# A perceiver layer on one core: attention scores taken in two halves, softmax sums from a separate product with ones

## The chip, the core and the metric

The kernel runs on one core of a Trainium2 chip. The metric is device time in microseconds of one execution, as the median of several runs. Five engines work side by side, each through its own queue in order: TensorE (PE, matmuls; its weight loads are listed as PEld), VectorE (DVE), ScalarE (ACT), GpSimd (POOL) and SyncE (SP, which here only issues DMAs). Matmuls write to PSUM, eight banks of 512 float32 values per partition; DVE and ACT read it there.

## What is computed

64 samples, each with 64 tokens of 256 features (x) and a context of 256 tokens (ctx). Cut to what matters here:

```python
def xattn(queries, ctx):            # 16 heads of 16 features
    q = (queries @ Wq.T + bq).reshape(B, L, H, E)
    k = (ctx @ Wk.T + bk).reshape(B, S, H, E)
    v = (ctx @ Wv.T + bv).reshape(B, S, H, E)
    scores = einsum('blhe,bshe->bhls', q, k)
    attn = softmax(scores * E ** -0.5, axis=-1)
    return einsum('bhls,bshe->blhe', attn, v).reshape(B, L, H * E) @ Wo.T + bo

x = x + xattn(layernorm(x), ctx)
x = x + causal_self_attention(layernorm(x))
x = x + ffn(layernorm(x))           # gate, up, down; integer weights and rows
```

All attention matmuls are in float32.

## The kernel before

Everything is written as operations in a graph (`Graph.op`, L165): engine, a planned duration, a due time (`at`), what is read and written, and a function that emits the instructions. `Graph.run` (L214) then plays a list schedule with those planned durations. At each step it lets the operation start that can start first, among those due soon (`AHEAD`), by due time and a few penalties (`LATE`, `TURN`). The order it finds is the order of each engine's queue. `SHIFT` and `LAST` (L126, L145) move due times by kind of operation. Buffers come from rings with so many slots (`RINGS`, L1071); an operation that needs a buffer waits until a slot is free. Semaphores are placed afterwards, from what each instruction reads and writes.

The samples are cut into nine groups (seven of 8, two of 4). For each pair of samples, `project` (L585) makes keys and values from the context (`keys` L511, `values` L517; matmuls at L491 and L526). For each sample, `cross` (L594) does the cross-attention. For each group, `prepare` (L563) normalises x and makes the queries; when the group's samples are done, `self_attention` (L709) and `ffn` (L865) follow, interleaved with the next group's cross-attention by due times.

One sample in `cross`, with 2 chunks of 128 features (`hg`, KC = 2) and 4 column or row tiles of 32 (`j`, NJ = 4). A tile of 32 features holds two heads, and the queries are stored twice, masked to one head or the other, so 128 query columns stand for 2 heads x 64 tokens.

1. `scT` (L614, PE): transposed scores of keys against queries, 2 chunks x 2 key blocks x 4 row tiles = 16 matmuls of 128 columns, into one PSUM buffer `sc` of four banks. The ring has one slot; `mm`, the ring of all other matmul outputs, has the other four banks.
2. `nm` (L623, DVE): one transposing reduce over all 2048 elements gives the maximum over 32 keys.
3. `larger` (L628, DVE, tile `msl`), `mtp` (L634, PE, a transpose) and `terms` (L645 to L649, DVE, tiles `less` and `mT`): the maximum per query, negated, and split into three bfloat16 terms with its rounding remainders.
4. `less` (L660, PE): bfloat16 matmuls with a selection matrix subtract the maxima from the scores in PSUM.
5. `exp` (L665, ACT), one per chunk, writes `PT`.
6. `av` (L673, PE): product with the values. The value tile is laid out per head as 16 value columns beside 16 columns of ones (the tiles `v_0`, `v_1` are filled with ones at L1049, and the copy at L532 writes only the value columns), so 32 weight columns give one head's result and its sum of probabilities at once. Each half of the query columns (`h`) has its own matmuls:

```python
nc.tensor.matmul(
    av.t[rows(j), h, hg, :],
    v.t[:, ((n % 2) * SC + s) * NP + hg * NJ + j, 2 * h:2 * h + 2, :].rearrange(
        "p a e -> p (a e)"),
    pT.t[:, hg, j, s, h * T:(h + 1) * T], start=(s == 0), stop=(s == SC - 1))
```

7. `keep` (L690) and `own` (L693) on ACT, `both` (L696) on POOL collect results and sums. `ratio` (L700, L701, DVE) moves the sums by 16 partitions with a shuffle and inverts them, and `yT` (L704, POOL) multiplies.

The self-attention scores (`ssc`, L747) use the same four-bank buffer `sc`, eight samples at a time; four masks (L759, DVE) read it.

Of the kernel before, what the change touches and what calls it, by code (L numbers as in the profile page):

```python
# [33 lines left out]
F32 = mybir.dt.float32  # L34
BF16 = mybir.dt.bfloat16
AF = mybir.ActivationFunctionType
# [10 lines left out]
NP = H // 2  # L47
# [50 lines left out]
class Op:  # L98
# [17 lines left out]
AHEAD = 6.1849  # L116
HURRY, SPURT = 3.4019, 8
WAIT = 2308970000.0
LATE = 0.0053
TURN = 3.4322  # L120
# [6 lines left out]
    "ACT exp": -1.4, "ACT hqT f": -5.46, "ACT hscaled f": 4.84, "ACT k a": -0.61, "ACT k s": 2.17,  # L127
    "ACT keep": 0.44, "ACT norm a": -1.22, "ACT norm f": 1.09, "ACT norm s": -0.51, "ACT own": 0.44,
    "ACT q a": -3.14, "ACT q s": 1.22, "ACT qT f": -23.19, "ACT rounded f": -0.4, "ACT sexp s": -0.94,
    "ACT silu f": -0.21, "ACT skeep s": 2.53, "ACT spT s": -1.53, "ACT turned a": -1.95,  # L130
    "ACT turned s": -0.14, "ACT up f": 1.2, "ACT v a": -0.19, "ACT v s": 1.1, "DVE bo r": -6.72,
    "DVE hq f": -0.63, "DVE hscales f": 3.5, "DVE larger": -1.95, "DVE mask s": -0.49, "DVE ratio": 0.94,
    "DVE smax s": 1.13, "DVE stats a": -2.59, "DVE stats f": -2.72, "DVE stats s": -1.327,
    "DVE stot s": 0.63, "DVE syT s": -1.42, "DVE terms": -1.95, "DVE wdown sums": -6.1,
    "DVE wup sums": -2.9, "DVE wup unit": 0.26, "DVE x a": -3.34, "DVE x f": -0.15, "DVE x s": 1.86,
    "PE av": 1.72, "PE bo r": -2.99, "PE down f": 0.54, "PE k s": -0.72, "PE mtp": -0.83, "PE o a": -0.97,
    "PE o s": 0.94, "PE q a": -0.32, "PE q s": -0.26, "PE qtp f": 3.25, "PE sav s": 1.22, "PE scT": 0.36,
    "PE ssc": -2.15, "PE turn a": -1.44, "PE v a": -0.32, "PE v s": 1.99, "PE wdown total": -3.1,
    "PE wgate total": -2.28, "PE wup total": -4.23, "POOL bias": 0.57, "POOL less s": -2.32,
    "POOL over s": 2.24, "POOL root a": -5.86, "POOL root f": -3.26, "POOL yT": 1.48, "SP hqT f": 4.97,  # L140
    "SP load wdown": -3.38, "SP load wk": 3.07, "SP load wq": 2.43, "SP load wup": -1.71, "SP load x": 2.01,
    "SP store": 4.49,
# [3 lines left out]
    "ACT hqT f": 5.73, "ACT hscaled f": -4.23, "ACT k s": -3.91, "ACT norm f": -4.37, "ACT norm s": -1.11,  # L146
    "ACT qT f": 22.14, "ACT rounded f": -3.05, "ACT skeep s": -6.38, "ACT spT s": -1.93,
    "ACT turned s": -2.39, "ACT up f": -1.39, "DVE hq f": 1.46, "DVE hscales f": 1.38, "DVE mask s": -1.14,
    "DVE q f": 2.07, "DVE smax s": -3.22, "DVE stot s": -2.49, "DVE syT s": -0.48, "DVE x f": 5.34,
    "PE down f": 5.04, "PE gate/up f": 3.79, "PE k s": 0.78, "PE q s": 0.23, "PE qtp f": -4.38,  # L150
    "PE stp s": -2.34, "POOL h f": 0.75, "POOL less s": 1.71, "POOL root f": 3.94,
}
END = 60.9419
# [7 lines left out]
class Graph:  # L161
# [52 lines left out]
    def run(self, emit=True):  # L214
# [13 lines left out]
        table, mode, landed = None, "", 0.0  # L228
# [27 lines left out]
        while len(done) < len(self.ops):  # L256
# [21 lines left out]
            for o in head.chain:  # L278
# [18 lines left out]
                if o.bytes:  # L297
                    landed = max(landed, t + 1900.0) + o.bytes / 330.0
# [40 lines left out]
def layers(nc, a, out, R, c):  # L339
# [6 lines left out]
    wk, wv, wq, wo, wqkv, wout = (Buf(t=c["w" + n]) for n in ("k", "v", "q", "o", "qkv", "out"))  # L346
    xs = [bufs("x", [P, GB[g] * T // P, D], f"x_{g}") for g in range(NG)]
    cTs, kTs, vs, qms, yTs = {}, {}, {}, {}, {}
    msl = [Buf(t=c[f"msl_{i}"][:, :, 0:3 * QB].rearrange("p a (b t) -> p a b t", t=3)) for i in range(2)]
    spread = [Buf(t=c[f"v_{i}"], shape=[P, 2 * SC]) for i in range(2)]  # L350
# [13 lines left out]
    def load_weights(at, w, name):  # L364
        op("SP", 60, at, f"load {name}", lambda: nc.sync.dma_start(w.t, a[name]), writes=[w],
           size=KC * D * 4 * P)
# [150 lines left out]
    def values(at, w, c0, src, name, v, i0, spread=False):  # L517

# [11 lines left out]
        def keep():  # L530
            if spread:
                nc.scalar.copy(v.t[:, i0 * NP:(i0 + k) * NP, 0::3, :],  # L532
                               pm.t[:, 0:k * D].rearrange("p (r h e) -> p r h e", h=2, e=E))
            else:
                nc.scalar.copy(v.t[:, i0:i0 + k, :],
                               pm.t[:, 0:k * D].rearrange("p (i d) -> p i d", d=D))

        op("PE", k * KC * pe(D) + 60, at, f"v {name}", emit, reads=[src, w], writes=[pm],
           holds=[] if spread else [v])
        op("ACT", act(k * D), at, f"v {name}", keep, reads=[pm], writes=[(v, i0)])  # L540
# [44 lines left out]
    def project(bp, at, step):  # L585

        kT = kTs[bp] = bufs("kT", [P, KC, 2 * S], f"kT_{bp}")
        v = vs[bp] = spread[bp % 2]
        for hg in range(KC):
            keys(at + step * hg, wk, 0, c["bk_c"][:, hg:hg + 1], cTs[bp], f"a{bp}", kT, hg)  # L590
        for i0 in (0, 2):
            values(at + step * (2 + i0 // 2), wv, 0, cTs[bp], f"a{bp}", v, i0, True)

    def cross(n, at):  # L594
# [5 lines left out]
        ms = msl[n % 2]  # L600
        sT = bufs("sc", [P, NJ, KC, S], f"scT_{n}")
# [7 lines left out]
        def scores():  # L609

            for hg in range(KC):
# [536 lines left out]
```

## Time and profile before

| what | value |
|---|---|
| median of 3 runs (lowest to highest) | 893.63 us (889.04 to 896.21) |
| the profiled execution's own time | 889.85 us |
| its span in the trace | 887.8 us |
| mean granted TensorE clock | 0.969 of full speed |
| ACT busy | 655.1 us, 74% |
| POOL busy | 428.5 us, 48% |
| share of the chain that ended last | PE 45%, DVE 37%, ACT 9%, POOL 3% |
| PE `k_a`, `v_a` busy | 126.0 us, 123.4 us |
| PE `scT`, `av` busy | 76.8 us, 71.3 us |
| DVE `nm` | 64 x 2307 ns, 147.6 us |

The profile is one execution. A group's row gives line, engine and operation, output and input by name, shapes and count; then busy microseconds and the mean of one in ns; then the idle time of the engine just before it and what ended that. Matmuls are pipelined, so the mean of one is its time from issue to result, and a block is shorter than count times mean. A busy PE is not a PE at its peak.

### The profile page before, as it was taken

How to read it: one execution, taken by the hardware profiler on the slowest of the kernel's cores; microseconds unless marked ns; L12 is line 12 of the kernel's file. 1: busy time of each engine (PE TensorE's matmuls, PEld its weight loads, DVE VectorE, ACT ScalarE, POOL GpSimd, SP SyncE). 2: the span in 40 equal slices, each digit the busy share in tenths (PEclk: the TensorE clock that was granted, in tenths of full speed). 3: DMA queues.
4: the chain of work that ended last, by engine and by line, in shares of the span. 5: the costliest groups of instructions: out<-in, count | busy, mean ns of one | idle time of the engine just before them, and what ended most of it. 6: DMA issues, size and time to landing. Idle time of an engine off the chain costs nothing.

```text
span 887.8 us, 26233 instructions
## 1 busy us (share of the span) xinstructions
PE 806.7 (91%) x11112; PEld 537.6 (61%) x11112; DVE 681.5 (77%) x1403; ACT 655.1 (74%) x1046; POOL 428.5 (48%) x633
## 2 busy tenths in 40 slices
PE   6988989989989999999999999999999998887866
PEld 4654656765557655676567655766566655666534
DVE  2567778777779967898589967898488768888775
ACT  2544556566987689877997689867787497857886
POOL 3423265424655245534475355534367136536764
PEclk8998999999999999999999999999899999989988
DMA  7121210010211221113121221012112030002111
GB/s 270 35 97 49 73 49 25 12 40 2 61 37 38 50 83 29 23 32 74 55 37 38 49 73 33 18 38 72 37 28 45 16 70 4 14 3 38 37 36 60
DMA packets 47876, 41.70 MB, mean 47 GB/s; under 512 B 39312, under 2 KB 39824, under 8 KB 47760
## 3 DMA queue, kind: packets, MB, share of 16 engines
q1 hardware_dynamic: 46176, 39.85, 16.7%
q8 instruction: 88, 1.44, 0.7%
q10 hardware_dynamic: 1584, 0.18, 0.1%
q14 instruction: 28, 0.23, 0.1%
HBM read 26.65 MB, written 4.19 MB: 35 GB/s over the span
## 4 chain that ended last, share of the span: by engine, by line
PE 45%; DVE 37%; ACT 9%; POOL 3%; issue 3%; DMA 3%; ACTq 0%; SPq 0%; POOLq 0%; DVEq 0%
DVE nm L623 8%; PE k_a L491 8%; PE scT L614 5%; PE v_a L526 5%; DVE s_s L759 3%; DVE smax_s L762 3%; PE q_a L491 3%; ACT PT L665 3%; PE av L673 3%; DVE stot_s L770 3%; DVE less L648 3%; PE k_s L491 3%; PE down_f L944 2%; DVE less L647 2%; DVE keep L701 2%
## 5 line engine op out<-in xcount | busy, mean ns | idle before, releaser
L623 DVE TRANSPOSE_TENSOR_REDUCE nm<-scT 128x64 f32<-128x2048 f32 x64 | 147.6, 2307 | 56.6 <-PE scT L614 56.2
L665 ACT ACTIVATE PT<-scT 128x1024 f32<-128x1024 f32 x128 | 124.1, 1022 | 79.5 <-PE scT L660 79.3
L491 PE MATMUL k_a<-cT,wk 128*128 128x512 f32 x256 | 126.0, 620 | 0.7 <-DMA wk<-in_wk_dram 0.7
L526 PE MATMUL v_a<-wv,cT 128*128 128x256 f32 x512 | 123.4, 385 | 0.8 <-DMA wv<-in_wv_dram 0.8
L918 POOL TENSOR_TENSOR h_f<-h_f,silu_f 128x512 f32<-128x512 f32 x64 | 81.6, 1285 | 55.3 <-ACT silu_f L912 34.3
L526 PEld LDWEIGHTS v_a<-wv,cT 128*128 128x128 f32 x512 | 93.5, 190 | 16.5 <-issue 1.5
L696 POOL TENSOR_TENSOR keep<-keep,own 128x256 f32<-128x256 f32 x64 | 47.3, 739 | 91.8 <-ACT own L693 91.5
L774 POOL TENSOR_TENSOR s_s<-s_s,stot_s 128x512 f32<-128x512 f32 (+1 forms) x72 | 67.8, 955 | 34.6 <-DVE stot_s L771 34.0
L764 POOL TENSOR_TENSOR s_s<-s_s,smax_s 128x512 f32<-128x512 f32 (+1 forms) x72 | 66.9, 956 | 34.0 <-DVE smax_s L762 31.1
L614 PEld LDWEIGHTS scT<-qm,kT 32*128 32x128 f32 x2048 | 64.5, 190 | 28.6 <-issue 15.2
L614 PE MATMUL scT<-qm,kT 32*128 32x128 f32 x2048 | 76.8, 287 | 1.8 <-ACT PT L665 1.7
L704 POOL TENSOR_TENSOR yT_a<-keep 128x128 f32<-128x128 f32 x64 | 31.0, 485 | 97.1 <-DVE keep L701 87.4
L673 PE MATMUL av<-PT,v 128*32 128x64 f32 x4096 | 71.3, 221 | 2.0 <-issue 0.9
L491 PEld LDWEIGHTS k_a<-cT,wk 128*128 128x128 f32 x256 | 46.4, 197 | 43.3 <-issue 36.2
L673 PEld LDWEIGHTS av<-PT,v 128*32 128x32 f32 x4096 | 60.5, 110 | 17.0 <-issue 7.9
L701 DVE RECIPROCAL keep<-keep 128x128 f32<-128x128 f32 x64 | 61.0, 953 | 2.2
L514 ACT ACTIVATE kT<-k_a,bk_c 128x512 f32<-128x512 f32 x64 | 43.4, 690 | 24.3 <-PE k_a L491 24.2
L759 DVE TENSOR_TENSOR s_s<-ssc,causal 128x512 f32<-128x512 f32 (+1 forms) x72 | 40.7, 619 | 20.5 <-PE ssc L747 20.5
L660 PE MATMUL scT<-mT,sel 32*128 32x256 bf16 x512 | 25.9, 276 | 28.6 <-DVE mT L649 28.4
L690 ACT ACTIVATE keep<-av,par 128x256 f32<-128x256 f32 x64 | 30.2, 472 | 27.4 <-PE av L673 27.4
L532 ACT COPY v<-v_a 128x512 f32<-128x512 f32 x64 | 37.2, 590 | 15.2 <-PE v_a L526 15.2
L841 DVE TENSOR_REDUCE amax_hf<-h_f 128x1 f32<-128x1024 f32 x32 | 38.4, 1201 | 12.7 <-POOL h_f L918 12.6
(156 smaller groups left out, 1773.8 us busy)
## 6 DMA issues: line engine op xcount, KB each, us to landing
cT<-in_ctx_dram SPq DMA_DIRECT2D x32, 512.0 KB, 3.7
x<-in_x_dram SPq DMA_DIRECT2D x7, 512.0 KB, 5.3
out_dram<-x SPq DMA_DIRECT2D x7, 512.0 KB, 2.7
wffn_gate<-in_wgate_dram SPq DMA_DIRECT2D x2, 512.0 KB, 4.5
wffn_up<-in_wup_dram SPq DMA_DIRECT2D x2, 512.0 KB, 5.5
wffn_down<-in_wdown_dram SPq DMA_DIRECT2D x2, 512.0 KB, 4.0
wqkv<-in_wqkv_dram SPq DMA_DIRECT2D x1, 768.0 KB, 7.3
x<-in_x_dram SPq DMA_DIRECT2D x2, 256.0 KB, 3.4
```

The lines of the kernel that those rows point to most:

```text
L491: nc.tensor.matmul(pm.t[:, 0:n], w.t[:, kc, c0:c0 + P], src.t[:, kc, :], start=(kc == 0), stop=(kc == KC - 1))
L526: nc.tensor.matmul(pm.t[:, i * D:(i + 1) * D], src.t[:, kc, (i0 + i) * P:(i0 + i + 1) * P], w.t[:, kc, c0:c0 + D], start=(kc == 0), stop=( ...
L614: nc.tensor.matmul(sT.t[:, j, hg, s * P:(s + 1) * P], kT.t[rows(j), hg, k0 + s * P:k0 + (s + 1) * P], q(hg, j), start=(hg == s == 0), stop ...
L623: op("DVE", dve(NJ * KC * S), at, f"nm {n}", lambda: nc.vector.tensor_reduce(nm.t.rearrange("p a s b -> p (a s b)"), sT.t.rearrange("p j c ...
L665: op("ACT", act(NJ * S), at + .03, f"exp {n}", lambda: nc.scalar.activation(pT.t[:, hg].rearrange("p j k n -> p j (k n)"), sT.t[:, :, hg, ...
L673: nc.tensor.matmul(av.t[rows(j), h, hg, :], v.t[:, ((n % 2) * SC + s) * NP + hg * NJ + j, 2 * h:2 * h + 2, :].rearrange("p a e -> p (a e)" ...
L696: op("POOL", pool(2 * KC * T) + 100, at + .055, f"both {n}", lambda: nc.gpsimd.tensor_tensor(t.t, t.t, u.t, ALU.add), reads=[u], writes=[t])
L701: nc.vector.reciprocal(t.t[:, 1], t.t[:, 1])
L759: op("DVE", dve(nt), p(k), f"mask {nm}", lambda: nc.vector.tensor_tensor(t.t, sc.t[:, j, 0:nt].rearrange("p (b k) -> p b k", k=T), c["caus ...
L764: op("POOL", pool(nt), p(k), f"less {nm}", lambda: nc.gpsimd.tensor_tensor(t.t, t.t, mx.t.unsqueeze(2).to_broadcast(full), ALU.subtract), ...
L774: op("POOL", pool(nt), p(k + 1), f"over {nm}", lambda: nc.gpsimd.tensor_tensor(t.t, t.t, tot.t.unsqueeze(2).to_broadcast(full), ALU.mult), ...
L918: op("POOL", pool(512), p(k), f"h {nm}", lambda: nc.gpsimd.tensor_tensor(h.t[:, n0:n0 + 512], h.t[:, n0:n0 + 512], sl.t, ALU.mult), reads= ...
```

## The change

- The scores buffer is one four-bank tile cut into two slots, each half of every bank. `scT`, `nm` and `exp` each work on one chunk in one slot, so a sample has two `scT` blocks of 8 matmuls and two `nm` of 1024 elements. [...] The self-attention scores are made four samples at a time, and each mask becomes two.
- `terms`: the maximum stays in PSUM, and two bitwise ANDs with integer masks (`cut`) and one subtraction give the three terms. `ms` has four entries per block of queries instead of three, so the constant-zero padding goes.
- Values are stored densely in a ring of three slots. `av` takes all 128 query columns of a tile, once with 32 value columns and once with 32 columns of ones; the shuffle in `ratio` goes. `keep` and `own` take the two halves of the queries.
- `kT` has three slots instead of two.
- The planner's constants, the offsets in `SHIFT` and `LAST` and several planned durations are other numbers.

```diff
-AHEAD = 6.1849
-HURRY, SPURT = 3.4019, 8
-WAIT = 2308970000.0
-LATE = 0.0053
-TURN = 3.4322
+AHEAD = 6.7367
+HURRY, SPURT = 2.6734, 8
+WAIT = 13355.2
+LATE = 0.0079
+TURN = 4.3354
...
-        ms = msl[n % 2]
-        sT = bufs("sc", [P, NJ, KC, S], f"scT_{n}")
+        sT = [bufs("sc", [P, NJ, S], f"scT_{n}_{hg}") for hg in range(KC)]
...
-        def scores():
-            for hg in range(KC):
-                for s in range(SC):
-                    for j in range(NJ):
-                        nc.tensor.matmul(sT.t[:, j, hg, s * P:(s + 1) * P],
-                                         kT.t[rows(j), hg, k0 + s * P:k0 + (s + 1) * P], q(hg, j),
-                                         start=(hg == s == 0), stop=False,
-                                         skip_group_check=True)
-        both = [(qm, (hg, h)) for hg in range(KC) for h in range(2)]
-        op("PE", KC * SC * pe(P) + 57, at, f"scT {n}", scores, reads=both + [kT], writes=[sT], mode="rows")
-        nm = bufs("nm", [P, NJ * KC, SC, QB], f"nm_{n}")
-        op("DVE", dve(NJ * KC * S), at, f"nm {n}", lambda: nc.vector.tensor_reduce(
-            nm.t.rearrange("p a s b -> p (a s b)"),
-            sT.t.rearrange("p j c (b q) -> p (j c b) q", q=32), AX.X, ALU.max, apply_transpose=True),
-           reads=[sT], writes=[nm])
-        op("DVE", 230, at + .01, f"larger {n}", lambda: nc.vector.tensor_tensor(
-            ms.t, nm.t[:, :, 0, :].unsqueeze(3).to_broadcast([P, NJ * KC, QB, 3]),
-            nm.t[:, :, 1, :].unsqueeze(3).to_broadcast([P, NJ * KC, QB, 3]), ALU.max),
+        def scores(hg):
+            for s in range(SC):
+                for j in range(NJ):
+                    nc.tensor.matmul(sT[hg].t[:, j, s * P:(s + 1) * P],
+                                     kT.t[rows(j), hg, k0 + s * P:k0 + (s + 1) * P], q(hg, j),
+                                     start=(hg == s == 0), stop=False, skip_group_check=True)
+        clear = bufs("clear", None, f"clear_{n}")
+        nm = bufs("nm", [P, NJ, KC, SC * QB], f"nm_{n}")
+        for hg in range(KC):
+            op("PE", SC * pe(P) + 80, at, f"scT {n}", lambda hg=hg: scores(hg),
+               reads=[(qm, (hg, h)) for h in range(2)] + [kT] + [clear] * hg,
+               writes=[sT[hg]] + [clear] * (not hg), mode="rows")
+            op("DVE", dve(NJ * S), at, f"nm {n}", lambda hg=hg: nc.vector.tensor_reduce(
+                nm.t[:, :, hg, :], sT[hg].t.rearrange("p j (b q) -> p j b q", q=32), AX.X, ALU.max,
+                apply_transpose=True), reads=[sT[hg]], writes=[(nm, hg)])
+        ms = bufs("ms", [P, NJ * KC, QB, 4], f"ms_{n}")
+        op("DVE", 300, at + .01, f"larger {n}", lambda: nc.vector.tensor_tensor(
+            ms.t, *(nm.t.rearrange("p j c k -> p (j c) k")[:, :, s * QB:(s + 1) * QB].unsqueeze(3).to_broadcast(
+                [P, NJ * KC, QB, 4]) for s in range(SC)), ALU.max),
            reads=[nm], writes=[ms])
...
-            pt.t[:, 0:P], c[f"msl_{n % 2}"].rearrange("p a s -> p (a s)"), c["ident"]), reads=[ms],
-           writes=[pt], holds=[mT])
-        less = bufs("less", [P, 2, 32], f"less_{n}")
+            pt.t[:, 0:P], ms.t.rearrange("p a b t -> p (a b t)"), c["ident"]), reads=[ms], writes=[pt],
+           holds=[mT])
+        cut = bufs("less", [P, QB, 32], f"less_{n}", I32)
         def terms():
-            y, z = less.t[:, 0], less.t[:, 1]
-            upper = lambda t: t.bitcast(BF16)[:, 1::2]
-            stt = nc.vector.scalar_tensor_tensor
+            y = pt.t[:, 2 * P:2 * P + 32]
+            u = pt.t[:, 3 * P:4 * P]
             nc.vector.tensor_reduce(y, pt.t[:, 0:P].rearrange("p (g q) -> p q g", q=32), AX.X, ALU.max,
                                     negate=True)
-            stt(z, upper(y), c["termpar"][:, 0:1], y, ALU.mult, ALU.add)
-            stt(y, upper(z), c["termpar"][:, 1:2], z, ALU.mult, ALU.add)
-            stt(mT.t, upper(y).unsqueeze(1).to_broadcast([P, QB, 32]), 1.0,
-                c["termpar"][:, 2:2 + QB].unsqueeze(2).to_broadcast([P, QB, 32]), ALU.mult, ALU.mult)
-        op("DVE", 200 + 2 * 200 + 300, at + .02, f"terms {n}", terms, reads=[pt], writes=[less, mT])
+            for i, d in enumerate((u.bitcast(I32).rearrange("p (b q) -> p b q", q=32), cut.t)):
+                nc.vector.tensor_tensor(d, y.bitcast(I32).unsqueeze(1).to_broadcast([P, QB, 32]),
+                                        c["cut"][:, i, :].unsqueeze(2).to_broadcast([P, QB, 32]),
+                                        ALU.bitwise_and)
+            nc.vector.tensor_tensor(mT.t.rearrange("p b q -> p (b q)"), u,
+                                    cut.t.rearrange("p b q -> p (b q)").bitcast(F32), ALU.subtract)
+        op("DVE", 1090, at + .02, f"terms {n}", terms, reads=[pt], writes=[cut, mT])
         pT = bufs("PT", [P, KC, NJ, SC, P], f"PT_{n}")
-        av = bufs("mm", [P, 2, KC, T], f"av_{n}")
+        av = bufs("mm", [P, 2, KC, 2, T], f"av_{n}")
         t = bufs("keep", [P, 2, KC, T], f"keep_{n}")
...
-                    nc.tensor.matmul(sT.t[:, j, hg, :], c["sel"][rows(j), hg, :],
+                    nc.tensor.matmul(sT[hg].t[:, j, :], c["sel"][rows(j), hg, :],
                                      mT.t[rows(j)].rearrange("p b q -> p (b q)").unsqueeze(1).to_broadcast(
                                          [2 * E, SC, P]), start=False, stop=True, skip_group_check=True)
         def probabilities(hg):
             op("ACT", act(NJ * S), at + .03, f"exp {n}", lambda: nc.scalar.activation(
-                pT.t[:, hg].rearrange("p j k n -> p j (k n)"), sT.t[:, :, hg, :], AF.Exp), reads=[sT],
+                pT.t[:, hg].rearrange("p j k n -> p j (k n)"), sT[hg].t, AF.Exp), reads=[sT[hg]],
                writes=[(pT, hg)], table="exp")
         def products(hg):
-            for h in range(2):
-                for s in range(SC):
+            for s in range(SC):
+                for k in range(2):
                     for j in range(NJ):
+                        d0 = hg * P + 2 * E * j
                         nc.tensor.matmul(
-                            av.t[rows(j), h, hg, :],
-                            v.t[:, ((n % 2) * SC + s) * NP + hg * NJ + j, 2 * h:2 * h + 2, :].rearrange(
-                                "p a e -> p (a e)"),
-                            pT.t[:, hg, j, s, h * T:(h + 1) * T], start=(s == 0), stop=(s == SC - 1))
-        op("PE", KC * pe(S, BF16) + 40, at + .03, f"less {n}", without, reads=[mT], writes=[sT], mode="rows",
+                            av.t[rows(j), k, hg, :, :].rearrange("p h q -> p (h q)"),
+                            c["ones"][:, 0:2 * E] if k else v.t[:, (n % 2) * SC + s, d0:d0 + 2 * E],
+                            pT.t[:, hg, j, s, :], start=(s == k == 0), stop=(s == SC - 1),
+                            skip_group_check=True)
+        op("PE", KC * pe(S, BF16) + 40, at + .03, f"less {n}", without, reads=[mT, clear], writes=sT, mode="rows",
            holds=[pT])
...
-            o = op("PE", SC * pe(P) + 114, at + .04, f"av {n}", lambda hg=hg: products(hg),
+            o = op("PE", 490, at + .04, f"av {n}", lambda hg=hg: products(hg),
...
-        op("ACT", act(2 * KC * T) + 100, at + .05, f"keep {n}", lambda: nc.scalar.activation(
-            t.t.rearrange("p h c q -> p h (c q)"), av.t[:, ::-1].rearrange("p h c q -> p h (c q)"),
-            AF.Copy, scale=c["par"][:, 1:2]), reads=[av], writes=[t])
-        op("ACT", act(2 * KC * T) + 100, at + .05, f"own {n}", lambda: nc.scalar.activation(
-            u.t.rearrange("p h c q -> p (h c q)"), av.t.rearrange("p h c q -> p (h c q)"),
-            AF.Copy, scale=c["par"][:, 0:1]), reads=[av], writes=[u])
-        op("POOL", pool(2 * KC * T) + 100, at + .055, f"both {n}", lambda: nc.gpsimd.tensor_tensor(
+        def keep(h, b, name):
+            op("ACT", act(2 * KC * T) + 100, at + .05, f"{name} {n}", lambda: nc.scalar.activation(
+                b.t.rearrange("p k c q -> p (k c) q"),
+                av.t[:, :, :, h, :].rearrange("p k c q -> p (k c) q"), AF.Copy, scale=c["par"][:, h:h + 1]),
+               reads=[av], writes=[b])
+        keep(1, t, "keep")
+        keep(0, u, "own")
+        op("POOL", pool(2 * KC * T) + 180, at + .055, f"both {n}", lambda: nc.gpsimd.tensor_tensor(
             t.t, t.t, u.t, ALU.add), reads=[u], writes=[t])
-        def ratio():
-            nc.vector.stream_shuffle(t.t[:, 1], t.t[:, 1], [(k + E) % (2 * E) for k in range(2 * E)])
-            nc.vector.reciprocal(t.t[:, 1], t.t[:, 1])
-        op("DVE", 294 + 953, at + .06, f"ratio {n}", ratio, reads=[], writes=[t])
+        op("DVE", 880, at + .06, f"ratio {n}", lambda: nc.vector.reciprocal(t.t[:, 1], t.t[:, 1]),
+           reads=[], writes=[t])
...
         def scores(hg, k):
-            sc = bufs("sc", [P, NJ, KC * S], f"ssc_{g}_{hg}")
             ts = [bufs("s", [P, gb, T], f"s_{nm}_{hg}_{j}", spare=("PT",)) for j in range(NJ)]
-            def emit():
-                for b in range(gb):
-                    for j in range(NJ):
-                        r = slice(2 * E * j, 2 * E * (j + 1))
-                        nc.tensor.matmul(sc.t[:, j, b * T:(b + 1) * T],
-                                         qm.t[r, hg, b, :, :].rearrange("p h q -> p (h q)"),
-                                         kT.t[r, hg, b * T:(b + 1) * T], start=True, stop=True)
-            op("PE", gb * 222, p(k), f"ssc {g}", emit,
-               reads=[(qm, (hg, 0)), (qm, (hg, 1)), (kT, hg)], writes=[sc], mode="rows", holds=ts)
+            def some(b0):
+                sc = bufs("sc", [P, NJ, S], f"ssc_{g}_{hg}_{b0}")
+                def emit():
+                    for b in range(b0, b0 + 4):
+                        for j in range(NJ):
+                            r = slice(2 * E * j, 2 * E * (j + 1))
+                            nc.tensor.matmul(sc.t[:, j, (b - b0) * T:(b - b0 + 1) * T],
+                                             qm.t[r, hg, b, :, :].rearrange("p h q -> p (h q)"),
+                                             kT.t[r, hg, b * T:(b + 1) * T], start=True, stop=True)
+                op("PE", 4 * 222, p(k), f"ssc {g}", emit,
+                   reads=[(qm, (hg, 0)), (qm, (hg, 1)), (kT, hg)],
+                   writes=[sc, bufs("clear", None, f"clear_{g}_{hg}_{b0}")], mode="rows", holds=ts)
+                return sc
+            sc = [some(b0) for b0 in range(0, gb, 4)]
             return [softmax(hg, j, sc, ts[j], k + j / 8) for j in range(NJ)]
...
-            op("DVE", dve(nt), p(k), f"mask {nm}", lambda: nc.vector.tensor_tensor(
-                t.t, sc.t[:, j, 0:nt].rearrange("p (b k) -> p b k", k=T),
-                c["causal"].unsqueeze(1).to_broadcast(full), ALU.add), reads=[sc], writes=[t])
+            for i, part in enumerate(sc):
+                op("DVE", dve(S), p(k), f"mask {nm}", lambda i=i, part=part: nc.vector.tensor_tensor(
+                    t.t[:, 4 * i:4 * i + 4, :], part.t[:, j, :].rearrange("p (b k) -> p b k", k=T),
+                    c["causal"].unsqueeze(1).to_broadcast([P, 4, T]), ALU.add), reads=[part], writes=[(t, i)])
...
-            op("POOL", pool(512), p(k), f"h {nm}", lambda: nc.gpsimd.tensor_tensor(
+            op("POOL", pool(512) + 230, p(k), f"h {nm}", lambda: nc.gpsimd.tensor_tensor(
                 h.t[:, n0:n0 + 512], h.t[:, n0:n0 + 512], sl.t, ALU.mult), reads=[sl], writes=[(h, n0)])
...
-    R = {name: Ring(ring(ps if name in ("mm", "sc") else sb, name), slots)
-         for name, slots in RINGS.items()}
+    R = {name: Ring(ring(ps if name == "mm" else sb, name), slots) for name, slots in RINGS.items()}
+    scores = ps.tile([P, NJ, 2 * S], F32, name="sc")
+    R["sc"].make = lambda k, b: scores[:, :, k * S:(k + 1) * S]
+    R["clear"].make = lambda k, b: None
...
-    "x": 5, "cT": 2, "kT": 2, "PT": 2, "qm": 2, "yT": 3, "xn": 2, "xnT": 2, "sqm": 1,
+    "x": 5, "cT": 2, "kT": 3, "v": 3, "PT": 2, "qm": 2, "yT": 3, "xn": 2, "xnT": 2, "sqm": 1,
...
-    "sc": 1, "mm": 4, "keep": 2, "own": 1, "skeep": 2, "mT": 2, "nm": 2, "less": 2, "mv": 4, "st": 4, "var": 4, "rstd": 4, "newton": 4,
+    "sc": 2, "clear": 1, "mm": 4, "keep": 2, "own": 1, "skeep": 2, "mT": 2, "nm": 2, "less": 1, "ms": 2, "mv": 4, "st": 4, "var": 4, "rstd": 4, "newton": 4,
...
```

## The prediction

> **What bounds the kernel now.** I read the busy line and the slices of the page first, then the windows, then the waits, then the chain, and last the groups for prices.
>
> ```profile
> span 887.8 us, 26233 instructions
> PE 806.7 (91%) x11112; PEld 537.6 (61%) x11112; DVE 681.5 (77%) x1403; ACT 655.1 (74%) x1046; POOL 428.5 (48%) x633
> ...
> PE   6988989989989999999999999999999998887866
> ```
>
> TensorE (PE) is nearly always at work, and the slices say where it is not: at the start and over the last fifth. The windows give this in microseconds (after the length: busy time of PE, weight loads, DVE, ACT and POOL, then the granted clock).
>
> ```profile
> 0.00:50.00 50.00, 43.33 (x342) 28.08 (x342) 21.04 (x48) 21.88 (x35) 18.88 (x33) 0.93 0.44 146
> 50.00:750.00 700.00, 654.16 (x9379) 433.79 (x9368) 555.17 (x1108) 527.38 (x829) 329.40 (x473) 0.99 0.17 43
> 750.00:887.80 137.80, 109.22 (x1408) 75.74 (x1406) 105.30 (x248) 105.81 (x184) 80.25 (x128) 0.90 0.13 30
> ```
>
> PE is idle for 6.7 us in the first window, 45.8 in the middle and 28.6 at the end, 81.1 in all. In the middle, where 56 or so of the 64 samples pass, it is 93% busy and DVE 79%. So PE's work is the bound there, and all that any other engine could give back is those 45.8 us. What are they made of?
>
> ```profile
> PE scT L660 <- DVE mT L649: 28.4, 30, 2.0
> PE mtp L634 <- DVE msl L628: 6.6, 10, 2.0
> ...
> PE scT L614 <- ACT PT L665: 1.7, 3, 1.0
> ```
>
> (Waiter, releaser: us in total, times, longest.) PE waits 35.0 us for DVE's chain of the maxima, and only 1.7 us for a free scores buffer. The change gives most of its effort to that buffer; the buffer is hardly waited for.
>
> **The product with the values: the large term.** Before, a sample has 2 chunks x 2 halves of the queries x 2 key blocks x 4 column tiles = 32 matmuls of 64 columns; each float32 matmul is two records, hence the x64 below. After, the loops are 2 chunks x 2 key blocks x 2 (values, then the constant) x 4 tiles: again 32, but each streams all 128 columns. Work per sample doubles, because the sums no longer ride along as weight columns beside the values. Three pieces of the chain price it:
>
> ```profile
> 404.22 1.10 PE scT L614 x32
> 405.32 1.03 PE av L673 x64
> 406.35 1.91 PE k_a L491 x4
> ...
> 408.38 1.72 PE k_a L491 x4
> ```
>
> Four column tiles run side by side, so the 64 records are 16 sets, one after another. Matmul by matmul, the sets of av start 55.8 ns apart, 16 x 55.8 = 0.89 us, and 1.03 - 0.89 = 0.14 us is fixed per block. The scores are 8 sets of four 128-column records, 111.8 ns apart once running (213 to the second one). So the new block is 16 x 111.8 + 140 = 1.93 us against 1.03: +0.90 us. From below: k_a streams 4 x 512 columns in 1.72 us, 0.84 ns a column, and each column tile must take its 16 x 128 columns in turn, 1.72 us, +0.69. From above: by the scores' whole block, 1.10 / 8 x 16 = 2.20 us, +1.17. I take +0.90, since the sets run on without a break. Times 64: **+57.3 us** (44 to 75), all on PE, which has no cover for it. The plan books 490 ns per chunk, 0.98 us a sample; if the trace is right, PE falls behind its plan by 0.95 us in every sample.
>
> **Split blocks.** The first set of a scores block costs 213 - 112 = 100 ns extra. Two blocks a sample pay it twice if something comes between: 64 x 0.1, and 14 of the 18 self-attention score blocks likewise, 1.4: 0 to 7.8 us, I take **+4**.
>
> **DVE, off the bound.**
>
> ```profile
> L648 DVE SCALAR_TENSOR_TENSOR less<-less,termpar 128x32 f32<-128x32 bf16 x64 | 29.2, 457 | 2.3
> ...
> L647 DVE SCALAR_TENSOR_TENSOR less<-less,termpar 128x32 f32<-128x32 bf16 x64 | 27.6, 432 | 2.3
> L649 DVE SCALAR_TENSOR_TENSOR mT<-less,termpar 128x128 bf16<-128x128 bf16 x64 | 26.4, 412 | 2.2
> L628 DVE TENSOR_TENSOR msl<-nm 128x96 f32<-128x96 f32 x64 | 24.8, 387 | 2.1
> ```
>
> The terms take 263 (the maximum, L645) + 432 + 457 + 412 = 1564 ns. Three of the four have short medians (252, 252 and 292 ns) and tails past 1100 ns, so something holds them up now and then. [...] The new three 128-element instructions each take one operand from PSUM. [...] The shuffle goes (-0.31). The maxima in two halves: the reduce of 1024 elements nearest to them (L841) takes 1.20 us, two are 2.40 against 2.31: +0.09. The larger-of-two grows from 96 to 128 elements, a third of 387 ns at the very most: +0.03 to 0.13. Per sample -0.6, times 64 = -38; the masks of 56 blocks fall in two, 2 x 416 against 677 ns: +9. DVE loses about 30 of 681 us. At 79% in the middle this shortens nothing by itself; it counts only through the 35.0 us that PE waits.
>
> **ACT, POOL and SP.** exp, keep and own have the same sizes and counts; the value copy loses its stride, and the unstrided one (sv) takes 588 ns against 590. The two memsets of the values (3.5 us on POOL, in the first microseconds) lie beside the first loads. No DMA is added. The third slot for keys and values lets projections go earlier; no wait of PE for such a slot stands among its waits, so I give it nothing of its own. All of it is covered by PE; without that cover it would be worth a few us at most.
>
> **What PE's waits give back.** After the change the last half of the scores needs only 1.2 us of reduce instead of 2.3 before the maxima are done, and the terms are 0.4 shorter: 1.5 us off a chain whose longest waits are 2.0, and PE has 0.9 us more other work to put before it. Most of the 35.0 should go, and some of the other 10.8; but the fixed order is laid out for a PE that is faster than it will be, so not all. I take **-25** (0 to -40).
>
> **A wait the change may add.** The two halves of the scores now share each bank. [...] No row of this trace shows two engines in one bank. [...] In the trace the next scores begin 1.08 us after the second exp ends in the median, and under 1.02 us in 31 of 63 cases: with the buffer this seldom pressed, the guard costs between 0 and 63 x 1.02 / 2 = 32 us. I take **+5**, because PE's own lag gives exp time to finish.
>
> **The sum.** 887.8 + 57.3 + 4 - 25 + 5 = 929.1 us of span. The profiled execution took 889.85 us, 2.1 over its span, and the median of the runs is 893.63, so 5.8 over the span: **935 us**, 4.6% slower.
>
> **The rivals.**
> [...]
> - *All the idle of the middle goes.* 929 - 5 - (45.8 - 25) = 903 of span, 909 us; with a better end, whose 28.6 us idle comes from the last group's own chain, 900. For it: chain and slots are both eased. Against: a fixed order at 93% seldom reaches 100%. It alone doesn't reach the time before.
> - *The other side: the wider stream is free.* If loading the weights and not streaming paces av (its 64 loads take 0.94 us of a 1.10 us block in the timeline), 128 columns cost what 64 do, as the plan's 490 ns has it. Then 887.8 + 4 - 25 + 5 + 5.8 = 878 us. It decides from the block of a sample staying under 1.03 + 16 / 64 = 1.28 us. [...]
>
> **How the numbers follow.** My forecast has 0.66 (own range 906 to 955), the guard 0.20 (945 to 980), all idle gone 0.08 (898 to 910), the free stream 0.06 (865 to 890). Differences within 1% cannot be told from none here. Faster by over 1% is the free stream, 0.06; within 1% is half of the third case, 0.04; slower 0.90. Leaving out the free stream, most of the third case and the guard's upper part gives 906 to 970 us.
>
> **What would show it.** Right: the av group near 123 us busy on PE instead of 71.3, a block of x64 at about 1.9 us, PE above 860 us in all and its wait for mT under 10 us; DVE near 650. Wrong: an av block near 1.0 us, or PE idle in the middle of more than 46 us, with a wait of the scores for PT (exp) at its head; that would be the guard.

## The result and the profile after

The changed kernel takes 916.48 us (median of 4 runs, 915.18 to 918.75) against 891.76 us for the kernel before in the same comparison: 1.0275 times as long, 95% interval 1.0224 to 1.0326. The forecast was 935 us with a range of 906 to 970: slower as said, by 25 us and not by 41. The sum was made for the span: 929.1 us, and the trace has 915.0.

The page of the changed kernel, read as that of the kernel before was:

```profile
span 915.0 us, 26202 instructions
PE 850.5 (93%) x11112; PEld 578.8 (63%) x11112; DVE 661.2 (72%) x1395; ACT 648.4 (71%) x1040; POOL 424.9 (46%) x629
...
PE   8998999999989999899999999899999998898866
```

PE is 44 us busier and still the bound; DVE is 20 us less busy. The windows of the changed kernel (columns as before):

```profile
0.00:50.00 50.00, 46.71 (x371) 31.19 (x371) 20.79 (x56) 23.07 (x37) 9.89 (x28) 1.00 0.46 148
50.00:750.00 700.00, 669.20 (x9089) 457.29 (x9089) 516.05 (x1054) 496.51 (x785) 318.69 (x457) 1.00 0.16 41
750.00:915.00 165.00, 134.59 (x1654) 90.31 (x1652) 124.41 (x287) 128.84 (x219) 96.29 (x145) 0.97 0.14 32
```

PE's idle time is now 3.3, 30.8 and 30.4 us, 64.5 in all instead of 81.1. The granted clock, ahead of the last two columns, is 1.00, 1.00 and 0.97, where the three windows before had 0.93, 0.99 and 0.90. The clock row of each page's slices shows the same, first the kernel before:

```profile
PEclk8998999999999999999999999999899999989988
```

and the changed one, where only one slice is below 9:

```profile
PEclk9999999999999999999999999999999999999989
```

This was no part of the forecast. The chain of the changed kernel has the new product's price (start, length, then the piece):

```profile
406.67 1.09 PE sav L801 x64
407.76 1.89 PE av L667 x64
...
414.48 1.10 PE sc L603 x32
```

The block that took 1.03 us takes 1.89. The waits of PE have changed places:

```profile
PE sc L603 <- ACT PT L657: 9.4, 13, 1.2
PE sc L603 <- DVE s_s L759: 9.1, 13, 1.3
PE mtp L625 <- DVE ms L619: 7.3, 12, 0.9
PE sc L742 <- ACT PT L657: 5.8, 7, 1.0
...
PE sc L652 <- DVE mT L641: 1.3, 2, 0.8
```

The wait for the terms (`mT`) fell from 28.4 us to 1.3. In its place PE waits ahead of scores for a buffer: for exp (`PT`), and for the causal masks of the self-attention (`s_s`). Last, DVE's groups with shapes kept apart:

```profile
L614 DVE TRANSPOSE_TENSOR_REDUCE nm<-sc 128x32 f32<-128x1024 f32 x128 | 154.1, 1229 | 84.1 <-PE sc L603 70.4 <-ACT xn_f L883 5.4 <-ACT qm L501 3.9
...
L619 DVE TENSOR_TENSOR ms<-nm 128x128 f32<-128x128 f32 x64 | 30.1, 471 | 2.1
L638 DVE TENSOR_TENSOR mtp<-mtp,cut 128x128 int32<-128x128 int32 x64 | 19.2, 300 | 2.2
L635 DVE TENSOR_REDUCE mtp<-mtp 128x32 f32<-128x128 f32 x64 | 18.8, 293 | 36.2 <-PE mtp L625 35.9
L638 DVE TENSOR_TENSOR less<-mtp,cut 128x128 int32<-128x128 int32 x64 | 18.6, 291 | 2.2
L641 DVE TENSOR_TENSOR mT<-mtp,less 128x128 bf16<-128x128 f32 x64 | 18.6, 291 | 2.2
```

The terms now take 293 + 300 + 291 + 291 = 1175 ns instead of 1564.

### The profile page after: what moved, and what is told of

Same layout as the page of the kernel before. It is cut to its first block, busy times and chain, and to the rows that moved or that the text cites. A ratio compares the mean times of both kernels' runs of the same rounds, so it can differ in the third digit from the quotient of the medians.

```text
span 915.0 us, 26202 instructions
## 1 busy us (share of the span) xinstructions
PE 850.5 (93%) x11112; PEld 578.8 (63%) x11112; DVE 661.2 (72%) x1395; ACT 648.4 (71%) x1040; POOL 424.9 (46%) x629
## 4 chain that ended last, share of the span: by engine, by line
PE 68%; DVE 14%; ACT 11%; issue 3%; DMA 2%; POOL 1%; DVEq 0%; ACTq 0%; POOLq 0%
PE av L667 13%; PE k_a L489 10%; PE sc L603 8%; PE v_a L523 8%; ACT PT L657 6%; DVE nm L614 5%; DVE s_s L759 4%; PE sc L742 4%; PE o_a L538 3%; PE o_s L538 3%; PE stp_s L782 2%; PE down_f L944 2%; PE k_s L489 2%; PE sc L652 2%; PE q_a L489 2%
## 5 line engine op out<-in xcount | busy, mean ns | idle before, releaser
L614 DVE TRANSPOSE_TENSOR_REDUCE nm<-sc 128x32 f32<-128x1024 f32 x128 | 154.1, 1229 | 84.1 <-PE sc L603 70.4
L657 ACT ACTIVATE PT<-sc 128x1024 f32<-128x1024 f32 x128 | 124.8, 1020 | 40.7 <-PE sc L652 32.8
L523 PEld LDWEIGHTS v_a<-wv,cT 128*128 128x128 f32 x512 | 94.8, 192 | 23.0 <-issue 10.1
L667 PE MATMUL av<-PT,v 128*32 128x128 f32 x2048 | 104.4, 276 | 0.4 <-ACT h_f L915 0.4
L667 PE MATMUL av<-PT,ones 128*32 128x128 f32 x2048 | 102.8, 273 | 0.0
L603 PE MATMUL sc<-qm,kT 32*128 32x128 f32 x2048 | 79.8, 286 | 21.3 <-ACT PT L657 9.4
L603 PEld LDWEIGHTS sc<-qm,kT 32*128 32x128 f32 x2048 | 64.4, 186 | 54.8 <-ACT PT L657 22.6
L759 DVE TENSOR_TENSOR s_s<-sc,causal 128x256 f32<-128x256 f32 x128 | 45.5, 418 | 56.3 <-PE sc L742 53.2
L686 ACT ACTIVATE own<-av,par 128x256 f32<-128x256 f32 x64 | 30.2, 472 | 63.3 <-PE av L667 62.8
L667 PEld LDWEIGHTS av<-PT,v 128*32 128x32 f32 x2048 | 56.0, 109 | 15.1 <-issue 7.8
L667 PEld LDWEIGHTS av<-PT,ones 128*32 128x32 f32 x2048 | 61.2, 110 | 0.0
```

What stands on the lines that cost most here:

```text
L523: nc.tensor.matmul(pm.t[:, i * D:(i + 1) * D], src.t[:, kc, (i0 + i) * P:(i0 + i + 1) * P], w.t[:, kc, c0:c0 + D], start=(kc == 0), stop=( ...
L603: nc.tensor.matmul(sT[hg].t[:, j, s * P:(s + 1) * P], kT.t[rows(j), hg, k0 + s * P:k0 + (s + 1) * P], q(hg, j), start=(hg == s == 0), stop ...
L614: op("DVE", dve(NJ * S), at, f"nm {n}", lambda hg=hg: nc.vector.tensor_reduce(nm.t[:, :, hg, :], sT[hg].t.rearrange("p j (b q) -> p j b q" ...
L657: op("ACT", act(NJ * S), at + .03, f"exp {n}", lambda: nc.scalar.activation(pT.t[:, hg].rearrange("p j k n -> p j (k n)"), sT[hg].t, AF.Ex ...
L667: nc.tensor.matmul(av.t[rows(j), k, hg, :, :].rearrange("p h q -> p (h q)"), c["ones"][:, 0:2 * E] if k else v.t[:, (n % 2) * SC + s, d0:d ...
L759: op("DVE", dve(S), p(k), f"mask {nm}", lambda i=i, part=part: nc.vector.tensor_tensor(t.t[:, 4 * i:4 * i + 4, :], part.t[:, j, :].rearran ...
```

## The experiments

The theory was that the wide product is the loss, nearly all of it paid on PE, and that part of it comes back as PE's waits for DVE shrink. Rivals: that the bank shared by the two halves costs the loss, and that the bit masks of the terms or the order of the queues matter more than the forecast allowed. The order needs care: it is made from planned durations, so an edit that changes one, or a number of slots, moves the whole order. "Same order" below means that the planned durations were left alone, or the order was written in as a list.

**The wide product.** First, in the changed kernel, the product streams only half of its columns; all else and the order stay.

```diff
-                            pT.t[:, hg, j, s, :], start=(s == k == 0), stop=(s == SC - 1),
+                            pT.t[:, hg, j, s, 0:T], start=(s == k == 0), stop=(s == SC - 1),
-                b.t.rearrange("p k c q -> p (k c) q"), av.t[:, :, :, h, :]...
+                b.t.rearrange("p k c q -> p (k c) q"), av.t[:, :, :, 0, :]...
```

> The changed kernel with every queue in the same order, but the product with values and ones streams 64 of the 128 query columns (the second half of each tile's queries is left out of the result; keep and own both read the first half). So only the stream of av goes back to its length before. Forecast's theory (PE's stream is the price): av blocks near 1.03 us instead of 1.89, 64 x 0.86 = 55 us less on PE, of which 10 to 15 us come back as PE waits: about 872 us (862 to 880). Rival, the bank guard decides: PE stops at the scores for the second exp and the masks; those waits grow by about what the stream gave, and the time stays above 890. Rival, the new order decides: 905 or more.

Measured: 873.27 us (ratio to before 0.978, 0.976 to 0.980), 43 us less than the changed kernel, as expected: most of the 54 us of stream is paid here, and the waits ahead of scores stayed at 10.1, 9.9 and 5.8 us. They are not an effect of the long product. Now the reverse: in the kernel before, only the product is made wide (dense values, 128 columns with values and with ones, no shuffle), same order.

```diff
-    pT.t[:, hg, j, s, h * T:(h + 1) * T], start=(s == 0), stop=(s == SC - 1))
+    pT.t[:, hg, j, s, :], start=(s == k == 0), stop=(s == SC - 1), skip_group_check=True)
-            nc.vector.stream_shuffle(t.t[:, 1], t.t[:, 1], [(k + E) % (2 * E) for k in range(2 * E)])
```

> The kernel before, with one part of the change alone: values stored densely, product over 128 columns with values and with ones, no shuffle; the planned durations, and so every queue's order, stay. Forecast's theory: 64 x 0.86 = 55 us more on PE, 10 to 20 of it taken from PE's idle: about 932 us (922 to 942), so more than the whole change. Rival, the stream is hidden in PE's waits and the other parts of the change cost the rest: 895 to 910.

Measured: 911.4 us, ratio 1.021 (1.019 to 1.023). A miss: the same stream costs only 18 us here. PE idles 13.9 us less (17.7 less with the records that its trace lacks, told under the table at the end), and half-clock time costs it 10.9 less. If that was slack being used up, a second helping must cost nearly its whole length:

```diff
-                for k in range(2):
+                for k in range(3):
-    c["ones"][:, 0:2 * E] if k else v.t[...]
+    c["half"][:, 0:2 * E] if k else v.t[...]
...
+    nc.gpsimd.memset(fixed("half", [P, 2 * E]), 0.5)
```

> The wide product in the kernel before (dense values, 128 columns, same order), with the product with the constant made twice, each with one half, so that a sample streams 1.5 times as much again: 64 x 16 / 2 x 111.8 ns = 57 us more on PE than the wide product alone (911.4 us), which cost only 18 of its 55. If PE's slack (idle, and time at half clock) is now used up: 911 + 45 to 57, so 956 to 968. If PE still takes two thirds out of slack: 925 to 935.

Measured: 960.07 us, ratio 1.075 (1.072 to 1.078), 48.7 us more than the wide product alone, of the 57 that were added to the stream, and within the expectation. Most of the slack had been used up.

**The bit masks of the terms.** In the kernel before, only the terms and the four entries per block of the new version, same order; then the reverse, the changed kernel with the old terms.

```diff
-            stt(z, upper(y), c["termpar"][:, 0:1], y, ALU.mult, ALU.add)
-            stt(y, upper(z), c["termpar"][:, 1:2], z, ALU.mult, ALU.add)
+                nc.vector.tensor_tensor(d, y.bitcast(I32).unsqueeze(1).to_broadcast([P, QB, 32]),
+                                        c["cut"][:, i, :].unsqueeze(2).to_broadcast([P, QB, 32]),
+                                        ALU.bitwise_and)
```

> The kernel before with one part of the change alone: the terms of the maxima by bit masks from PSUM (four entries per block of queries instead of three); product, scores, slots, planned durations and so every queue's order stay. Terms should fall from 1564 to about 1180 ns, as in the changed kernel. Forecast's theory (PE waits 28.4 us for mT, DVE's chain is shorter than the order assumes or near it): PE's wait for mT falls by a third to a half, 883 to 890 us. If PE's stream alone decides: no difference, 891 to 896.

> The changed kernel with the terms made as before (scalar_tensor_tensor from SBUF, 1.56 us instead of 1.18), in the same order of every queue; all else as changed. Forecast's theory: with the longer product PE has other work before it needs mT (its wait there is 1.3 us), so little comes back: 917 to 922 us. If the masks are what keeps PE's waits short: 925 to 935.

Measured: 863.55 us for the masks alone (861.04 to 866.51), ratio 0.968 (0.965 to 0.971), **the best kernel of this study**; and 940.29 us (ratio 1.052, 1.049 to 1.056) for the changed kernel without them. They gain 30 us in the one order (28 by the median that the table below takes for the kernel before) and 24 in the other, more than expected both times. The waits of the kernel with masks alone show where from:

```profile
PE scT L662 <- DVE mT L651: 9.3, 16, 1.4
PE mtp L635 <- DVE msl L629: 6.4, 12, 2.1
```

The wait for `mT` fell from 28.4 to 9.3 us.

**The halves, and the order.** Undoing the halves in the changed kernel, with the constants of its planner kept; and, with not one instruction changed, telling the planner the product's true duration:

```diff
-        sT = [bufs("sc", [P, NJ, S], f"scT_{n}_{hg}") for hg in range(KC)]
+        sT = bufs("sc", [P, NJ, KC, S], f"scT_{n}")
```

```diff
-            o = op("PE", 490, at + .04, f"av {n}", lambda hg=hg: products(hg),
+            o = op("PE", 950, at + .04, f"av {n}", lambda hg=hg: products(hg),
```

> The changed kernel with the halves undone: one scores buffer of four banks, one block of 16 matmuls, one maximum over 2048 elements, self-attention scores of eight samples at a time; masks for the terms, product with ones, third slots and constants stay. The order is planned anew. Forecast's theory (the halves are kept apart by bank, so they give next to nothing, and PE's stream bounds): 910 to 922 us. Rival, the halves' new waits (28.7 us of PE idle at the scores) are a cost of their own: 890 to 900. Third: the halves do give overlap: 925 to 940.

> The changed kernel with the planned duration of the product raised from 490 to 950 ns per chunk, near the 0.94 measured; the order is planned anew, nothing else changes. Forecast's theory (PE is bound by its stream, and 64.5 us of idle are left, of which a better plan could take some): 908 us (900 to 918). Rival, the wrong plan is the price: under 895. If the order was well tuned around the wrong figure: 918 to 930.

Measured: 955.84 us (ratio 1.070, 1.067 to 1.073) and 963.34 us (1.081, 1.077 to 1.084). Both are misses of the same sort. The second has only another order, and it costs 47 us; so the first says nothing about halves. Two more runs let the planner search its constants anew, first for the changed kernel without halves, then for halves and masks with the narrow product (two slots for keys and values, as the dense values had made the room for a third; the diff is the second run's).

```diff
-    "x": 5, "cT": 2, "kT": 3, "v": 3, "PT": 2,
+    "x": 5, "cT": 2, "kT": 2, "v": 2, "PT": 2,
...
-                            av.t[rows(j), k, hg, :, :].rearrange("p h q -> p (h q)"),
+                            av.t[rows(j), h, hg, :],
```

> The changed kernel with the halves undone as in the run that took 955.8 us, but with offsets and planner's constants searched anew on the kernel's own plan (planned end 830 us; 871 in that run, 809 in the changed kernel). If that run was slow through an order that no longer fitted: 915 to 935. If halves are worth 40 us by themselves: 945 to 960.

> The changed kernel with the product undone (ones beside the values, 64 columns) and, because dense values made the room for them, two slots for keys and values again; halves and masks stay; product planned at 515 ns a chunk, offsets and constants searched anew (planned end 827 us). Forecast's theory: like the run with half the columns, 873, or a little less if the new order is good: 860 to 880. Masks in the old order and old scores: 863.6. If halves are worth something: under 855.

Measured: 916.19 us (1.028, 1.024 to 1.032), the time of the changed kernel; and 888.21 us (0.996, 0.994 to 0.998), worse than expected and worse than the 863.55 of the masks with whole buffers in the old order. A replanned order isn't the same test twice, so the last two runs hold the old order. First the kernel before with the edits of the masks and of the wide product shown above, then all parts of the change, with each engine's queue as in that run (its edit is below: a slot for values is reserved no earlier than in the kernel before, and the order is read from a list).

> The kernel before with two parts of the change, the masks and the wide product, in the old order of every queue; no halves, no third slots, old constants. Masks alone gave 30 us, the wide product alone cost 18. If their sizes simply add: 881 us. Forecast's theory, sharpened by the runs so far (each draws on the same slack of PE, idle time and half clock; with less slack the stream is paid nearly in full): 863.6 + 40 to 50 = 904 to 914. What is then left to 916.5 is the price of halves, slots and new order together; if those give something, this run lies above 916.5.

> All parts of the change (halves of the scores banks, masks, wide product, third slots), but each engine's queue in the order of the kernel before: the order is that of the run with masks and wide product (896.9 us), with each scores block, maxima, self-attention scores block and mask replaced by its two halves, one directly behind the other. Before this run it was open whether the 19.5 us between that run and the changed kernel (916.5) are the halves or the new order. If the new order costs it, this run lands near 897 us (893 to 903). If the halves cost it (two blocks of scores, two reduces, the wait for the bank), it lands near 916 (911 to 921). Halves that help when the order is good would give under 890.

```diff
-           holds=[v])
+           holds=[] if name[0] == "a" else [v])
...
-            t, head = best
+            head = self.ops[ORDER[turn]]
+            turn += 1
+            t = start(head)
```

Measured: 896.94 us (1.0053, 1.003 to 1.0075), a miss between the two expectations, and 898.3 us (1.0084, 1.0055 to 1.0113), as expected if the new order costs the rest. The groups of scores on PE, first in the kernel before (the idle time stands behind the second bar):

```profile
L614 PE MATMUL scT<-qm,kT 32*128 32x128 f32 x2048 | 76.8, 287 | 1.8 <-ACT PT L665 1.7
L747 PE MATMUL ssc<-skT,sqm 32*128 32x64 f32 x1024 | 32.7, 273 | 0.1
```

in this last kernel:

```profile
L742 PE MATMUL sc<-qm,kT 32*128 32x128 f32 x2048 | 75.1, 283 | 2.3 <-ACT PT L796 2.2
L881 PE MATMUL sc<-skT,sqm 32*128 32x64 f32 x1024 | 32.7, 273 | 0.9 <-ACT PT L796 0.8
```

and in the changed kernel, with the same halves in its own order:

```profile
L603 PE MATMUL sc<-qm,kT 32*128 32x128 f32 x2048 | 79.8, 286 | 21.3 <-ACT PT L657 9.4 <-DVE s_s L759 9.1 <-DVE nm L614 1.5
L742 PE MATMUL sc<-skT,sqm 32*128 32x64 f32 x1024 | 34.7, 275 | 7.4 <-ACT PT L657 5.8 <-DVE s_s L759 0.6 <-ACT skT L512 0.3
```

The 28.7 us that PE idles ahead of scores are 3.2 in the old order.

## Why the forecast was right and where it was wrong

The four runs in one order take the change apart (medians; the kernel before had 890.6 to 893.6 from one comparison to the next, so a step of 3 us is none):

| kernel | us | step | span | PE busy | lost at half clock | PE idle: scores | maxima, terms | elsewhere |
|---|---|---|---|---|---|---|---|---|
| before | 891.8 | | 887.8 | 806.7 | 23.7 | 1.9 | 36.8 | 42.4 |
| + masks | 863.6 | -28.2 | 858.9 | 795.9 | 15.3 | 3.5 | 17.4 | 42.1 |
| + wide product | 896.9 | +33.4 | 895.5 | 841.5 | 14.6 | 4.1 | 12.0 | 37.9 |
| + halves, third slots | 898.3 | +1.4 | 896.4 | 847.1 | 15.4 | 3.2 | 11.6 | 34.5 |
| + new order (the change) | 916.5 | +18.2 | 915.0 | 850.5 | 6.8 | 28.7 | 10.6 | 25.2 |

"Lost at half clock" is half of PE's busy time inside the stretches where the record of the granted clock says 0.5, an upper bound; the idle columns are sums of group rows like those above, and PE busy and the three of them make the span. The traces of the second and third row, and that of the wide product alone, lack 38 of PE's 11112 records, all of gate and up projections. Without the same records the trace of the kernel before has 3.8 us less of PE busy, so in those rows PE busy is about that much too low and the idle time elsewhere too high.

*The product, +57.3: right.* Cut down to its tile, the trace has PE 71.32 us busy with it before and 125.08 after, +53.8; a block takes 1.89 us where 1.93 was worked out. The free stream is out. *Split blocks, +4: right*, 76.8 to 79.8 and 32.7 to 34.7 us, +5.0; in the old order, with the halves back to back, nothing of it is left.

*PE's waits, -25: right in what it named.* The waits ahead of the maxima's transposes and of `less` went from 36.8 to 10.6 us, -26.2. By the table the masks gave 19.4 of it, the longer product 5.4, and the halves, from which the forecast had most of its shorter chain (1.1 of 1.5 us a sample), only 0.4 in the old order. The other 0.4 us of that chain, and most of the 0.6 us a sample for DVE, are shorter terms; 263 + 3 x 292 = 1139 ns were taken for them, a figure that no run shows. In the trace they went from 1564 to 1175 ns, -0.39 us. The forecast of DVE's busy time, -30 us, came out at -20.3: two reduces of half the size cost 2458 ns and not 2400 (3.7 us in all), the terms 36 ns more than the 1139 (2.3 us), and `hq_f` (L936), which the forecast had unchanged, rose by 4.8 us. That such savings shorten nothing by themselves was right in mechanism, for they came through PE's wait for `mT`; but it hid the size. The masks alone are worth 28 us: 19 of idle time, and 8 of clock.

*The guard, +5: mis-sized.* By the guard the forecast means that the next sample's scores wait for the second exp, though the first has freed their half of the buffer. That they must was the author's assumption: no run shows such a rule, only what the waits were. Idle time ahead of scores grew by 26.8 us, where 0 to 32 was the range and 935 - 5 + 32 = 962 us the time if all of it came. In the trace of the changed kernel none of the 384 reads of the scores (maxima, exp, causal masks) overlaps with any of the 3584 matmul records that write them. In 28 of the 64 samples the next scores begin 52 or 53 ns after the end of the second exp, though the first exp, and with it one half of the buffer, was done at least 0.9 us earlier. In these 28 PE idles for 15.5 us after the end of the first exp (worked out from the starts and ends; 3.1 us in 9 samples in the old order). That much is the guard. Where scores do come between, the reader of the other half waits for them, as the causal masks do five times in DVE's waits:

```profile
DVE s_s L759 <- PE sc L603: 3.1, 5, 0.8
```

So in this trace the two halves take turns and never work side by side. Most of the rest is PE's 9.7 us of waiting for the causal masks, which the forecast did not have at all. The 962 us did not come, as other savings came with the wait, which that figure had not counted. And it takes the order to make the guard bite: in the old order PE waits 3.2 us ahead of the same halves. The reading that fits both is that the new order puts scores early, where only a half that is freed by itself would let them start, and that there they wait for the other half's reader, as in the 28 samples; no run tests it alone.

*Not in the sum: the clock and the remaining idle time.* After less before, on the span: busy time without the clock's loss +60.7 (forecast 57.3 + 4 = 61.3), clock -16.9 (forecast 0), idle -16.6 (forecast -25 + 5 = -20). These make +27.2, the measured difference; the forecast had +41.3. **The step that failed is that the clock was left out of it**: 14.1 us too much, of which 16.9 are the clock, -3.4 the idle time and 0.6 the work. By the table 8.4 us of the clock's gain came with the masks and 8.6 with the new order. The profiled execution had the highest mean clock of the four (0.992, the others 0.985 to 0.990), so 16.9 is at the upper end. Within the idle time two errors nearly cancel: 21.8 us more ahead of scores than was booked, 17.2 less elsewhere than before, where the forecast had no change. That was luck. The clock is also why one sign failed: PE is busy for 850.5 us, not above 860, since the work added 60.7 us and the clock took 16.9 back. The sign named for the guard came by half: scores waiting for `PT` head PE's waits, but the middle has 30.8 us of idle time, not more than 46.

*Slots and order, nothing: wrong for the order.* The third slots cost or bring nothing that shows, together with the halves 1.4 us in the old order. The forecast booked nothing for the order, which it named only as a reason to take -25 and not -35; it costs 18.2 us. Of these, 15.2 are idle time (+25.5 ahead of scores, -1.0 at the maxima, -9.3 elsewhere) and 3.4 busy time. Clear of the clock the busy time grew by 12: 6.7 of it is the rows of the scores, and where the rest lies was not settled. The plan behind the new order still books 0.98 us a sample for a product that takes 1.89.

**What stays open.** Whether halves in banks of their own would be free apart was not tried: the scores and `mm` take four banks each, all that the kernel has, and `mm` would have to give some up. So no run shows how much of the 25.5 us comes from sharing banks and how much from the press on two slots; the 15.5 us above are read from one trace. Another order may also make shared halves pay. The costs don't add: the product costs 18 us in the kernel before, 33 once the masks have taken the waits away, 43 in the changed kernel. The first difference is shared slack; the second was not taken apart.

## What to carry to other kernels

Price work that is added to the bound engine by its stream, and then ask how much idle and half-clock time it will fill: two edits that feed on the same slack don't add up (here the wide product cost 18 us alone and 33 behind the masks). Where the order is planned, hold it fixed to judge an edit, since another order of the same instructions moved the time by 47 us here, more than any one part of the change. And before half a buffer is counted as a second buffer, look in the trace whether its reader and the other half's writer ever overlap; here they never did, and the new order, whose plan frees each half by itself, left PE waiting.

## What the hardware showed

The granted clock was not the same in the two kernels. The trace of the kernel before records it at 0.5 for 54.6 us of the span, in which PE is busy for 47.5; that of the changed kernel for 14.1 us, with PE busy for 13.7. Their mean clocks are 0.969 and 0.992. Within each trace, of the three windows above, the one with the lowest clock is the one in which PE is least busy: 0.90 with PE 79% busy in the kernel before, 0.97 with 82% in the changed one.

The idle time in all does not decide it, though. By the table the kernel with masks and wide product has 54.0 us of it and loses 14.6 at half clock; the changed kernel has 64.5 and loses 6.8. The masks alone took the idle time from 81.1 to 63.0 us and the loss from 23.7 to 15.3, and the waits that they shortened were of at most 2.0 us each. That the shorter waits raised the clock was not shown; what lowers it stays open here.
